# Extra tiles that hold the norm times differences of gamma rows: one conditioning kernel, a new set of tiles for boundary tokens

## The chip, the core and the metric

The kernel runs on one core of a Trainium2 chip. The metric is the device time of one execution in microseconds (us), the median of several runs. The engines of the core work side by side, each through its own queue in order: TensorE (PE, matrix products; PEld is its weight load), VectorE (DVE), ScalarE (ACT), GpSimd (POOL), and SyncE (SP), which here only issues DMAs. POOL issues the indirect DMAs (gathers and scatters), too. An instruction at the head of a queue that waits for another engine or a transfer holds all those behind it.

## The reference

For 8192 tokens (16 batches of 512) of width 512, six vectors are made of each token's row, weighted by a softmax `w`, joined to 3072 columns, and sent through a two-layer perceptron with a norm. `c` is a compartment of 5, `m` a scale type (0 or 1 in the inputs, `mask_BxS_ik0`; the table has 3 rows):

```python
h = _ln(x, pw_g[pathway_ids], pw_b[pathway_ids])        # one of 500 rows
h = _ln(h, cp_g[compartment_ids], cp_b[compartment_ids])
t = _ln(x, tm_g[time_steps], tm_b[time_steps])          # time_steps = the compartment's index
m, n, r = x + cond_1, x + cond_2, x + cond_3            # rows of the batch
s = _ln(x, ms_g[scale_type], ms_b[scale_type])
cat = concatenate([w[0]*h, w[1]*t, w[2]*m, w[3]*n, w[4]*r, w[5]*s])
x = x + _ln(silu(cat @ int_W1 + int_b1) @ int_W2 + int_b2, int_g, int_be)
```

All of it is float32.

## The kernel before, in words

**Sorted tokens.** The kernel numbers the 15 groups (m, c) and sorts the tokens by group on the chip. Rows of x are fetched by gathers and the results scattered back, so a tile of 128 sorted tokens nearly always belongs to one group. 16 windows of 512 tokens (4 tiles) run one after the other. For a tile of one group, gamma of t and of s is one row each, so `t` and `s` share the plain norm `n` of x: `n @ V` with `V = diag(w1 tm_g[c]) W_t + diag(w5 ms_g[m]) W_s`. `s_part` (ACT, piece `sp`) makes the second summand, `build` (DVE, piece `bd`) adds the first, for each tile, into one of two buffers `vs`. The first layer of a tile is then three products of four chunks: `X` (x by `wx_`, the weighted sum of three blocks of `int_W1`), `V`, and `H` (the h path by `wh_`). The second layer is the product with `w2` (`Z`). What depends only on group and batch (betas, conditions, bias) is a row of a table (`rows_1`, `rows_2` in DRAM), gathered into tiles `add` by `i_add` (`gather_add`, piece `ga`) and added to the products in PSUM.

**Turning.** An operand goes through a 32x32 block transpose on DVE (`turn`, tiles `rX`, `rV`, `rH`, `rZ`) and then four DMAs per group of rows on SP (`spread_row`: `cX`, `cV`, `cH`, `cZ`).

**Boundary tokens.** Where a group ends inside a tile, the tile has tokens of two groups. Before the change the tile's V is that of the group that holds position 64 (`middle`), and tokens of the other group have their norm multiplied by 0 (`prim`, used in `x_mean` to make `mrs` and `mnm`, from which `norm_v` makes the masked norm; `norm_n` makes the plain one). The 14 boundaries give 14 half tiles of 64 positions, joined in pairs to `NX` = 7 extra tiles of 128 tokens, held as two extra windows `e0` (tiles 0 to 3) and `e1` (tiles 4 to 6). For them the kernel gathers x again (`gx.e*`), takes its norm, gathers both gamma rows of each token from `pair_rows` (`gather_pair`, `gr`), multiplies (`by_pair`, `mt`: two products a tile), turns both (`turn_pair`, `tr`), spreads both (`sT`, `sS`), multiplies with the weights `wt` and `ws` (`extra`, `ex`: 4 chunks each), adds the group's row of `rows_1` (`extra_add`, `ea`, a gather; `extra_end`, `ee`), and writes the sums behind the table in `rows_2` (`extra_out`, `eo`). Boundary tokens take their row from there. `of_begins`, `begins` and `swap_begins` (`bx`, `by`, `px`) compute where the boundaries lie; `extra_adds` (`xa`) and `add_rows` (`ar`) make the indices.

**The head.** Sorting ends at about 33 us. From there to the last product of window 1's H, and some way into window 2, a written-out sequence `ORDER` sets what every engine's queue gets. Each word is a call, as `lX.0.1` for layer 1, block X, window 0, tile 1. The others that the prediction names: `gh` gathers the h path's rows into `pw` and `cp` (three buffers each); `xs` sums x and its squares on ACT; `xe`, `xp`, `xm` make the norm's factors (DVE, POOL, DVE); `nv`, `xn` the norms; `tv`, `tx`, `tz` turn; `f1`, `fp`, `fm`, `fn`, `f2` are the h path's steps; `wk.s.c` adds a part to `wx_`; `h2`, `he`, `eh`, `cs`, `cp`, `cn`, `ct`, `ca`, `cm`, `cr` make the condition rows; `tb`, `br2` the beta rows (`tb` reads `wh_`, weighted by `wh` and loaded by `lh`); `pk`, `rp`, `rc`, `ro` make and write the table; `sz`, `scl` the scales of the tiles; `ax`, `ac`, `pwi`, `tk` the token indices; `sh` adds a row to x; `ha`, `hs` are the hidden layer's addition and silu; `l2` the Z product. After the head, `step` issues sixteen steps for each of the windows 2 to 14, and `last_window` the last.

Of the kernel before, what the change touches and what calls it, by code (L numbers as in the profile page):

```python
# [23 lines left out]
def kernel(ctx: ExitStack, tc: tile.TileContext, a: dict, out: bass.AP):  # L24
# [73 lines left out]
    prim = const.tile([P, NJ, NW], F32, name="prim")  # L98
# [98 lines left out]
    def x_mean(st):  # L197
        w = st["w"]
        st["nm"] = small.tile([P, NJ], F32, tag="nmx", name="nmx")
        nc.vector.tensor_mul(st["nm"], st["sums"][:, 1], st["rs"])  # L200
        for k in ("rs", "nm"):
            if isinstance(w, int):
                st["m" + k] = m = small.tile([P, NJ], F32, tag="m" + k, name="m" + k)
                nc.vector.tensor_mul(m, st[k], prim[:, :, w])
            else:
                st["m" + k] = st[k]

    def norm(st, j, rs, nm, tag):
        t = xnp.tile([P, D], F32, tag=tag, name=f"{tag}{st['w']}_{j}")
        nc.scalar.activation(t, st["xb"][:, j, :], AF.Identity, bias=st[nm][:, j : j + 1],  # L210
                             scale=st[rs][:, j : j + 1])
        return t
# [9 lines left out]
    def norm_v(st, j):  # L222
        st["xm", j] = norm(st, j, "mrs", "mnm", "xm")
# [4 lines left out]
    def norm_n(st, j):  # L228
        st["xn", j] = norm(st, j, "rs", "nm", "xn")
# [203 lines left out]
    i_half = iota(prep.tile([P, 2, NX], F32, name="i_half"), [[1, 2], [2, NX]])  # L433
# [141 lines left out]
    def half_cols(k):  # L575
# [15 lines left out]
        lambda: nc.gpsimd.tensor_add(half[:, :1], half[:, 1:], i_row[:NB]),  # L591
        lambda: nc.gpsimd.tensor_scalar(slot, i_half[:NB], i_row[:NB], half[:, :1], ALU.is_equal, ALU.mult),
    ]

    def tile_pairs():
        pt = ps_2.tile([P, 2, Q * NW], F32, tag="p2", name="ptp")
        for v, w in enumerate((wcs, wms)):
            nc.tensor.matmul(pt[:NR, v], w[:, :NR], middle, start=True, stop=True)
        p0 = ps_1.tile([P, Q + 1, NW], F32, tag="p1", name="p0")
        nc.tensor.matmul(p0[:, :Q].rearrange("p g w -> p (g w)"), ones[:NB], middle, start=True, stop=True)  # L600
        for g in range(Q):
            nc.tensor.matmul(p0[g * L : (g + 1) * L, Q], ones[:NB, :L], middle[:, g * NW : (g + 1) * NW],
                             start=True, stop=True)
        return pt, p0
# [7 lines left out]
    def row_pairs():  # L612
# [23 lines left out]
    at_c = scratch(0, P)[: Q * NW]  # L636
# [35 lines left out]
    HOME = {"e0T": "Z", "e0S": "X", "e1T": "Z", "e1S": "V"}  # L672
# [8 lines left out]
    def of_rows():  # L681

        at_["pa"] = pa = ps_2.tile([P, 3, Q * NW], F32, tag="p2", name="pa")
        nc.tensor.transpose(pa[:, 0], at_c, ident[: Q * NW, : Q * NW])
        swap(pa[:, 1:].rearrange("p v (j w) -> p j v w", j=NJ), at_n[:, 1:].rearrange("p v g w -> p g v w"), 2 * NW)
# [14 lines left out]
    def of_begins():  # L700

        at_["pnx"] = pnx = ps_2.tile([P, 2, NX], F32, tag="p2", name="pnx")
        H = P // 2
        for k in range(2):
            for h in range(2):
                nc.tensor.matmul(pnx[k * H : (k + 1) * H, 0], at_c[:, h * H : (h + 1) * H], b_at[:, h, k::2],
                                 start=(h == 0), stop=(h == 1))
# [12 lines left out]

# [51 lines left out]
    def rows_of_pw():  # L772
        nc.vector.tensor_scalar(i_pw, both, (1 << PW) - 1, None, ALU.bitwise_and)
        nc.vector.tensor_copy(i_cp.rearrange("p j w -> p (j w)"), at_["pa"][:, 2])
# [406 lines left out]
```

## Time and profile before

| what | us |
|---|---|
| median of 3 runs | 1024.62 |
| lowest and highest run | 1023.46 and 1024.70 |
| span of the profiled execution, first to last instruction | 1018.6 |
| PE busy in it | 987.3 |
| DVE busy | 827.9 |
| ACT busy | 547.2 |
| POOL busy | 554.0 |

The page gives the profiled execution's time only as this span; the runs' median is 6.0 us above it. The mean clock that was granted to PE is 0.991 of full speed. A matrix product of 128 x 128 by 128 x 512 in float32 stands as two instructions, so a tile's product with a 512 x 512 block is 8 of them. "Busy" of PE counts overlapping instructions once. In lines of waits, the engine before the arrow waited for what stands behind it; a row of the order of instructions has its start, its duration, engine, line, operation, operands, shape and count, and in brackets the idle time before it. Line numbers are those of the code above; L137 is `spread_row`, L169 `build`, L163 `s_part`, L278 `layer1`, L297 `layer2`, L890 `extra`, L878 `by_pair`, L103 any gather.

### The profile page before, as it was taken

The numbers are of one execution on the slowest core, as the hardware profiler recorded it, in microseconds if no ns is written. First come the engines' busy times: TensorE is split into PE (matmuls) and PEld (weight loads), VectorE is DVE, ScalarE is ACT, GpSimd is POOL, SyncE is SP. The second block draws the span as 40 slices with busy tenths as digits, with TensorE's granted clock in tenths as the row PEclk, the third lists the DMA queues.
The fourth block names the chain that finished last, engine by engine and source line by source line (L and its number), as shares of the span: only waits on it lengthen the run. The fifth ranks groups of instructions, "written<-read, shape, count | busy, mean of one in ns | idle before, by whom it ended". The sixth has DMA issues, their size and how long they took to land.

```text
span 1018.6 us, 10840 instructions
## 1 busy us (share of the span) xinstructions
PE 987.3 (97%) x2593; PEld 451.2 (44%) x2593; DVE 827.9 (81%) x1442; ACT 547.2 (54%) x1098; POOL 554.0 (54%) x561
## 2 busy tenths in 40 slices
PE   7998989899999999999999999999999999999996
PEld 7733434344444444444444444444444444444442
DVE  8698375888888888889888888888888889888844
ACT  5786634636464554736473746455463747364311
POOL 8437354537464655556564746464655656473514
PEclk9799999999999999999999999999999999999999
DMA  8858776767666666667685766667766768575412
GB/s 285 272 153 277 226 234 169 216 164 231 169 197 180 183 187 198 192 196 202 169 231 158 220 167 198 181 186 188 202 192 193 202 175 226 159 224 162 138 51 91
DMA packets 93505, 194.57 MB, mean 191 GB/s; under 512 B 25712, under 2 KB 25712, under 8 KB 93444
## 3 DMA queue, kind: packets, MB, share of 16 engines
q0 software_dynamic: 32048, 108.81, 36.3%
q1 hardware_dynamic: 60692, 85.00, 30.2%
q8 instruction: 22, 0.36, 0.1%
q14 instruction: 39, 0.32, 0.1%
q10 hardware_dynamic: 704, 0.08, 0.1%
HBM read 104.47 MB, written 19.67 MB: 122 GB/s over the span
## 4 chain that ended last, share of the span: by engine, by line
DVE 45%; DMA 13%; issue 13%; PE 9%; ACT 7%; SPq 6%; POOL 5%; POOLq 0%; DVEq 0%; ACTq 0%
DVE vs L169 13%; SPq L137 6%; DMA cH<-rH 5%; DVE yb L326 4%; DVE add L282 3%; POOL xbs L103 3%; PE p L278 3%; DVE pw L234 3%; DVE pw L262 3%; DVE sth L108 3%; DVE pw L233 3%; PE p L297 2%; PE pe L890 2%; ACT xn L210 2%; DVE rZ L129 2%
## 5 line engine op out<-in xcount | busy, mean ns | idle before, releaser
L297 PE MATMUL p<-w,cZ 128*128 128x512 f32 x512 | 229.0, 592 | 2.1 <-DMA cZ<-rZ 2.1
L278 PE MATMUL p<-vs,cV 128*128 128x512 f32 x504 | 226.8, 593 | 1.9 <-DVE vs L169 1.9
L278 PE MATMUL p<-wh__83,cH 128*128 128x512 f32 x512 | 223.0, 593 | 5.3 <-DMA cH<-rH 5.3
L278 PE MATMUL p<-wx__82,cX 128*128 128x512 f32 x512 | 222.9, 593 | 0.0
L169 DVE SCALAR_TENSOR_TENSOR vs<-wt,sct,vs 128x512 f32<-128x512 f32 x252 | 206.7, 879 | 0.0
L163 ACT ACTIVATE vs<-ws,scs 128x512 f32<-128x512 f32 x252 | 160.5, 707 | 0.3
L242 POOL TENSOR_TENSOR rsh<-veh,mhalf 128x1 f32<-128x1 f32 x64 | 45.7, 713 | 202.6 <-DVE veh L238 191.8
L278 PEld LDWEIGHTS p<-wh__83,cH 128*128 128x128 f32 x512 | 97.0, 190 | 128.6 <-issue 123.9
L297 PEld LDWEIGHTS p<-w,cZ 128*128 128x128 f32 x512 | 97.1, 190 | 125.3 <-issue 120.5
L278 PEld LDWEIGHTS p<-wx__82,cX 128*128 128x128 f32 x512 | 97.0, 190 | 122.7 <-issue 118.3
L278 PEld LDWEIGHTS p<-vs,cV 128*128 128x128 f32 x504 | 94.8, 190 | 124.8 <-issue 92.0
L249 ACT ACTIVATE pw<-pw,nmh,rsh 128x512 f32<-128x512 f32 x64 | 51.8, 810 | 125.3 <-DVE nmh L120 121.2
L285 ACT ACTIVATE add<-add 128x512 f32<-128x512 f32 x64 | 40.4, 631 | 144.9 <-DVE add L282 144.9
L331 POOL DMA_INDIRECT out<-yb,tok x64 | 70.0, 1093 | 71.1 <-DVE yb L326 24.5
L305 ACT ACTIVATE junk<-yb 128x512 f32<-128x512 f32 x64 | 40.1, 627 | 95.9 <-DVE yb L300 95.9
L103 POOL DMA_INDIRECT add<-rows,i_add x64 | 75.6, 1181 | 18.8 <-issue 12.4
L233 DVE TENSOR_TENSOR pw<-xn,pw 128x512 f32<-128x512 f32 x64 | 44.0, 687 | 51.3 <-ACT xn L210 49.0
L103 POOL DMA_INDIRECT xbs<-in_x,tok x64 | 64.4, 1006 | 35.1 <-issue 18.3
L267 POOL TENSOR_TENSOR xbs<-xbs,rows 128x512 f32<-128x512 f32 x64 | 81.5, 1274 | 0.9
L103 POOL DMA_INDIRECT pw<-in_pw,i_pw x64 | 63.8, 996 | 30.6 <-DVE rH L129 13.9
L210 ACT ACTIVATE xm<-xbs,mnm,mrs 128x512 f32<-128x512 f32 x64 | 48.7, 805 | 55.8 <-DVE rV L129 49.1
L103 POOL DMA_INDIRECT cp<-cp_rows,i_cp x64 | 65.1, 1017 | 19.9 <-issue 19.2
(255 smaller groups left out, 1145.2 us busy)
## 6 DMA issues: line engine op xcount, KB each, us to landing
cV<-rV SPq DMA_DIRECT2D x256, 64.0 KB
cH<-rH SPq DMA_DIRECT2D x256, 64.0 KB
cZ<-rZ SPq DMA_DIRECT2D x256, 64.0 KB
cX<-rX SPq DMA_DIRECT2D x240, 64.0 KB
w1x<-in_int_W SPq DMA_DIRECT2D x2, 1024.0 KB
cTe<-rTe SPq DMA_DIRECT2D x28, 64.0 KB
cSe<-rSe SPq DMA_DIRECT2D x28, 64.0 KB
rows<-adde SPq DMA_DIRECT2D x7, 256.0 KB
```

The costliest lines, as they stand in the source:

```text
L103: nc.gpsimd.indirect_dma_start(dst, None, table, bass.IndirectOffsetOnAxis(ap=idx, axis=0), **kw)
L137: nc.sync.dma_start(st[cat][q * L : (q + 1) * L, g].rearrange("p c t -> p (c t)"), st[rot][g * L : (g + 1) * L, q].rearrange("p c j t -> p ...
L163: nc.scalar.activation(v[:, c], ws[:, c], AF.Identity, scale=scs[:, c, g, w : w + 1])
L169: nc.vector.scalar_tensor_tensor(v[:, c], wt[:, c], sct[:, c, g, w : w + 1], v[:, c], ALU.mult, ALU.add)
L210: nc.scalar.activation(t, st["xb"][:, j, :], AF.Identity, bias=st[nm][:, j : j + 1], scale=st[rs][:, j : j + 1])
L233: nc.vector.tensor_mul(pw[:, :D], st.pop(("xn", j)), pw[:, :D])
L242: nc.gpsimd.tensor_tensor(rs, st.pop(("ve", j)), mhalf[:, :1], ALU.pow)
L249: nc.scalar.activation(pw[:, :D], pw[:, :D], AF.Identity, bias=st.pop(("nm", j)), scale=st.pop(("rs", j)))
L267: nc.gpsimd.tensor_add(st["xb"][:, j, :], st["xb"][:, j, :], rows[:, 2, :])
L278: nc.tensor.matmul(st["p1", g], st["c" + blk][:, g, c, :], m[:, c, :], start=(blk == "X" and c == 0), stop=(blk == "H" and c == NC - 1))
L297: nc.tensor.matmul(p2, st["cZ"][:, j, c, :], w2[:, c, :], start=(c == 0), stop=(c == NC - 1))
L331: nc.gpsimd.indirect_dma_start(out_rows, bass.IndirectOffsetOnAxis(ap=tok[:, j, w : w + 1], axis=0), yb[:, j, :], None)
```

## The change

The main V product takes all tokens of the tile with the plain norm, boundary tokens, too; so `prim` and the masked factors go, and one set of factors serves `norm_v` and `norm_n`. For tokens whose group differs from the tile's, the extra tiles now make the correction `n * (gamma row of its own - gamma row of the tile)`. The tokens that differ in compartment need the T block, those that differ in scale type the S block. Seven T tiles take the 14 half tiles, and one S tile takes the two boundaries at which the scale type changes (`b_at[:, :, :2]`). So there are eight extra tiles of one block each, where there were seven of two.

The differences are rows of a small table `diff_rows` (25 pairs of compartments and 9 of scale types), made by one product of `tg` (the eight gamma rows) with a matrix `picks` of +1 and -1 (`dk`, `dp`), copied with the weight (`dc`) and written to DRAM (`do`). `pair_rows` and its six DMAs go. `kinds` (`kd`) computes which pair each extra token has, from its own group and that of its tile (`g_at`, three more products in `row_pairs`).

The S tile (k = 0) is written behind the table in `rows_1`; the T tiles gather from `rows_1` with these rows included, so a token that differs in both adds its S correction to its T tile. `ORDER` is new throughout; of the pieces `prim` is gone, and `kd`, `dk`, `dp`, `dc`, `do` and `sE` come in.

The core of the diff:

```diff
-    rows_1 = dram.tile([NB1, D], F32, name="rows_1")
+    rows_1 = dram.tile([NB1 + P, D], F32, name="rows_1")
-    pair_rows = dram.tile([NG, 2 * D], F32, name="pair_rows")
+    diff_rows = dram.tile([ND, D], F32, name="diff_rows")
...
     def x_mean(st):
         nc.vector.tensor_mul(st["nm"], st["sums"][:, 1], st["rs"])
-        for k in ("rs", "nm"):
-            if isinstance(w, int):
-                st["m" + k] = m = small.tile([P, NJ], F32, tag="m" + k, name="m" + k)
-                nc.vector.tensor_mul(m, st[k], prim[:, :, w])
...
+        pgt = ps_2.tile([P, 3 * (P // 2)], F32, tag="p2", name="pgt")[: Q * NW]
+        nc.tensor.matmul(pgt[:, :P], cols[:, 6], rowed, start=True, stop=False)
+        nc.tensor.matmul(pgt[:, :P], cols[:, 5], ones[:NB], start=False, stop=True)
+        nc.tensor.matmul(pgt[:, P:], cols[:, 7], ones[:NB, : P // 2], start=True, stop=True)
...
+        for v, (src, lo, step) in enumerate(((at_c, 0, H), (g_at, 0, H), (g_at, P, 0))):
+            for k in range(2):
+                for h in range(2):
+                    nc.tensor.matmul(pnx[k * H : (k + 1) * H, v], src[:, lo + h * step :][:, :H], b_at[:, h, k::2],
+                                     start=(h == 0), stop=(h == 1))
...
+    def diff_product():
+        at_["pdr"] = pdr = psum(1, "pdr")[:ND]
+        nc.tensor.matmul(pdr, picks[:, 0], tg, start=True, stop=True)
...
-        st["r", j] = r = gp.tile([P, 2 * D], F32, tag="pw", name=f"pr{st['w']}_{j}")
-        gather(r, pair_rows[:, :], tok_x[:, j, 1, e : e + 1])
+        st["r", j] = r = gp.tile([P, D], F32, tag="cp", name=f"pr{st['w']}_{j}")
+        gather(r, diff_rows[:, :], tok_x[:, j, 1, e : e + 1])
+    def by_diff(st, j):
+        nc.vector.tensor_mul(st["r", j], st.pop(("xm", j)), st["r", j])
+    def turn_diff(st, j):
+        turn_to(st, "rE", HOME[st["w"] + "E"], j, st.pop(("r", j)))
...
-        for v, m in (("cT", wt), ("cS", ws)):
-            for c in range(NC):
-                nc.tensor.matmul(pe, st[v][:, k % Q, c, :], m[:, c, :],
-                                 start=(v == "cT" and c == 0), stop=(v == "cS" and c == NC - 1))
+        for c in range(NC):
+            nc.tensor.matmul(pe, ext[k // Q]["cE"][:, k % Q, c, :], (wt if k else ws)[:, c, :],
+                             start=(c == 0), stop=(c == NC - 1))
...
-        gather(at_["adde", k], rows_1[:, :], i_addx[:, k : k + 1])
+        gather(at_["adde", k], rows_1[: NB1 + (P if k else 0), :], i_addx[:, k : k + 1])
...
-        nc.sync.dma_start(rows_2[NB1 + k * P : NB1 + (k + 1) * P, :], at_["adde", k])
+        if k == 0:
+            nc.sync.dma_start(rows_1[NB1:, :], at_["adde", k])
+        else:
+            nc.sync.dma_start(rows_2[NB1 + (k - 1) * P : NB1 + k * P, :], at_["adde", k])
```

The new order, by queue, over the part from the sorting to the end of window 1's first layer, where the prediction speaks of it:

```
PE:   sz bx ax h2.1 h2.2 cv h2.0 eh.2 eh.0 px eh.1 dp xt.0.2 xt.0.3 xt.0.1 xt.0.0 ct tb cm lX.0.1 lX.0.3 lX.0.0 rp.1 lX.0.2 rp.0
      lV.0.1 lV.0.0 lH.0.1 lH.0.0 lV.0.3 lV.0.2 ex.0 ex.1 lH.0.3 ex.3 ex.2 ex.4 ex.6 ex.7 ex.5 lX.1.2 lX.1.3 lH.0.2 lX.1.0 lX.1.1
      lV.1.0 lV.1.1 lV.1.2 l2.0.1 l2.0.0 l2.0.2 l2.0.3 lV.1.3 lH.1.0 lH.1.1 lH.1.2 lH.1.3
DVE:  ... tk cg cs wk.2.2 xv.0.2 tt wk.2.0 cn xv.0.3 xe.0 xv.0.1 xv.0.0 xm.0 ca f1.0.2 wk.2.1 wk.2.3 fm.0.2 f1.0.0 tv.0.2 f2.0.2 ...
      ... ee.1 ee.2 ee.3 f1.1.3 ee.4 tv.1.1 fm.1.0 ee.6 bd.1.0 tv.1.2 ee.7 ee.5 tv.1.3 fm.1.3 f1.1.2 f2.1.0 fm.1.2 bd.1.1 ...
POOL: gh.0.2 gh.0.0 gh.0.1 cp gx.e1.3 gx.e0.1 gx.e1.2 xp.0 gx.e0.0 fp.0.2 ... gh.1.3 xp.1 ea.2 ea.1 gx.2.1 sh.0.3 ea.4 sh.1.0 ea.3 ea.6
      fp.1.0 gx.2.3 ea.7 fp.1.3 ea.5 sh.0.1 fp.1.2 ga.0.3 ga.0.2 ga.0.1 ga.0.0 ...
SP:   ... sE.e0.3 eo.0 sE.e1.0 sE.e1.2 sE.e1.3 sE.e1.1 eo.2 eo.1 sX.1.2 eo.3 sX.1.3 sH.0.2 sX.1.0 eo.6 eo.4 eo.7 eo.5 sX.1.1 sV.1.1 ...
```

Before, the same stretch of PE's queue was:

```
PE:   h2.1 bx ax sz px h2.0 xt.0.0 xt.0.1 xt.0.2 cv eh.0 xt.0.3 eh.1 h2.2 lX.0.1 eh.2 lX.0.2 lX.0.0 ct lX.0.3 cm tb lV.0.1 rp.0 rp.1
      lV.0.3 lV.0.0 lV.0.2 lH.0.0 lH.0.2 lH.0.1 ex.0 ex.1 ex.3 ex.2 lH.0.3 ex.6 ex.4 ex.5 lX.1.0 ... lX.1.3 lV.1.0 ... lV.1.3
      l2.0.1 l2.0.2 l2.0.0 l2.0.3 lH.1.0 lH.1.1 lH.1.2 lH.1.3
```

More of the change, by code (lines that the diff above doesn't have):

```diff
@@ L23 @@
+"""
 @with_exitstack
@@ L432 @@
     nc.gpsimd.tensor_scalar(i_own, i_own, float(NB1), None, ALU.add)
-    i_half = iota(prep.tile([P, 2, NX], F32, name="i_half"), [[1, 2], [2, NX]])
+    i_sx = prep.tile([P, 1], F32, name="i_sx")
+    nc.gpsimd.tensor_scalar(i_sx, i_row, float(P // 2), float(-(P // 2)), ALU.is_ge, ALU.mult)
+    nc.gpsimd.tensor_add(i_sx, i_sx, i_row)
+    nc.gpsimd.tensor_scalar(i_sx, i_sx, float(NB1), None, ALU.add)
+    picks = prep.tile([P, 2, ND], F32, name="picks")[:NR]
+    for v in range(2):
+        iota(picks[:, v, :ND5].rearrange("p (a b) -> p a b", a=NR5), [[1 - v, NR5], [v, NR5]])
+        iota(picks[:, v, ND5:].rearrange("p (a b) -> p a b", a=NR3), [[1 - v, NR3], [v, NR3]], base=NR5)
+    w_d = prep.tile([P, 1], F32, name="w_d")[:ND]
+    nc.gpsimd.tensor_scalar(w_d, i_row[:ND], float(ND5), None, ALU.is_ge)
     h1 = scratch(1, NC, 3, L)
@@ L598, in tile_pairs @@
             nc.tensor.matmul(pt[:NR, v], w[:, :NR], middle, start=True, stop=True)
[L599 to L603, printed above, removed]
+        p0 = ps_1.tile([P, Q, NW], F32, tag="p1", name="p0")
+        nc.tensor.matmul(p0.rearrange("p g w -> p (g w)"), ones[:NB], middle, start=True, stop=True)
         return pt, p0
@@ L719, in extra_tokens, with diff_picks, diff_copy, diff_out @@
         nc.vector.tensor_scalar(tok_x[:, :, 0], tok_x[:, :, 0], PW, None, ALU.logical_shift_right)
+    def diff_picks():
+        pk = picks[:, 0]
+        nc.vector.tensor_scalar(pk, pk, i_row[:NR], None, ALU.is_equal)
+        nc.vector.scalar_tensor_tensor(pk, picks[:, 1], i_row[:NR], pk, ALU.is_equal, ALU.subtract)
+        dw = small.tile([P, 1], F32, tag="dw", name="dw", bufs=1)[:ND]
+        nc.vector.tensor_sub(dw, wx[:ND, 5:6], wx[:ND, 1:2])
+        nc.vector.scalar_tensor_tensor(w_d, w_d, dw, wx[:ND, 1:2], ALU.mult, ALU.add)
+    def diff_product():
+        at_["pdr"] = pdr = psum(1, "pdr")[:ND]
+        nc.tensor.matmul(pdr, picks[:, 0], tg, start=True, stop=True)
+    def diff_copy():
+        at_["dr"] = gp.tile([P, D], F32, tag="add", name="dr", bufs=4)[:ND]
+        nc.scalar.activation(at_["dr"], at_["pdr"], AF.Identity, scale=w_d)
+    def diff_out():
+        nc.sync.dma_start(diff_rows[:, :], at_["dr"])
     def x_block(s, c):
```

141 lines of the change are left out of this document (86 added, 55 removed).

## The prediction

> **What bounds the kernel now.** I read the page first (the span, the engines' shares, the slices), then the busy time by stretches, then the waits of TensorE (PE) in the first 260 us, then the order of instructions on PE, VectorE (DVE), ScalarE (ACT), GpSimd (POOL) and SyncE's DMA queue (SP) in the head. The page:
>
> ```profile
> span 1018.6 us, 10840 instructions
> PE 987.3 (97%) x2593; PEld 451.2 (44%) x2593; DVE 827.9 (81%) x1442; ACT 547.2 (54%) x1098; POOL 554.0 (54%) x561
> ```
>
> PE leaves only 31 us of the span idle. The stretches say where; the columns are the stretch, PE, PEld, DVE, ACT and POOL busy (instructions), clock, DMA share, GB/s:
>
> ```profile
> 32.40:91.80 59.40, 58.37 (x331) 28.99 (x331) 48.97 (x111) 43.47 (x94) 30.01 (x30) 0.91 0.67 209
> 91.80:107.90 16.10, 10.83 (x25) 4.54 (x26) 7.74 (x19) 9.61 (x25) 11.81 (x12) 1.00 1.04 319
> 107.90:165.80 57.90, 53.32 (x122) 23.31 (x120) 31.42 (x57) 26.96 (x57) 23.57 (x23) 0.97 0.67 197
> 165.80:224.50 58.70, 55.70 (x129) 24.06 (x128) 47.98 (x84) 31.05 (x59) 30.25 (x31) 1.00 0.70 191
> 224.50:960.00 735.50, 734.98 (x1713) 324.50 (x1712) 633.57 (x1079) 407.39 (x793) 418.76 (x398) 1.00 0.68 191
> ```
>
> From 224.5 us on PE runs without a gap: 1713 instructions in 735.5 us, 0.429 us each. The change does not touch that code except for two tiny DVE products a window. So the time moves by what happens to the end of the head, the last H product of window 1 (lH.1.3), which ends here at 224.5. The PE instructions that I use, by start, duration, line and operands:
>
> ```profile
> 36.58 0.39 PE L706 MATMUL pnx<-b_at,room 64*64 64x7 f32 x4
> 37.66 0.36 PE L684 MATMUL pa<-ident,room 64*128 64x64 f32 x1
> 51.03 3.70 PE L278 MATMUL p<-wx__82,cX 128*128 128x512 f32 x8
> 71.78 3.70 PE L278 MATMUL p<-vs,cV 128*128 128x512 f32 x8
> 75.32 1.02 PE L855 MATMUL pr<-br,pick 128*120 128x512 f32 x2
> 80.50 7.03 PE L278 MATMUL p<-vs,cV 128*128 128x512 f32 x16
> 104.35 3.67 PE L278 MATMUL p<-wh__83,cH 128*128 128x512 f32 x8 [3.19 <-DMA cH<-rH]
> 107.86 3.60 PE L890 MATMUL pe<-wt,cTe 128*128 128x512 f32 x8
> 111.29 3.60 PE L890 MATMUL pe<-ws,cSe 128*128 128x512 f32 x8
> 143.50 5.30 PE L890 MATMUL pe<-wt,cTe 128*128 128x512 f32 x8 [4.58 <-DMA cTe<-rTe]
> 148.63 3.60 PE L890 MATMUL pe<-ws,cSe 128*128 128x512 f32 x8
> ```
>
> One product of a 128-token tile with one 512x512 block is 8 instructions and takes 111.29 - 107.86 = 3.43 us. PE's waits in the head (total, times, longest), leaving out those before 33 us, in code that hardly changes:
>
> ```profile
> PE p L278 <- DMA cH<-rH: 5.3, 2, 3.2
> PE pe L890 <- DMA cTe<-rTe: 4.6, 1, 4.6
> PE p L297 <- DMA cZ<-rZ: 2.1, 2, 1.7
> PE p L278 <- DVE vs L169: 1.4, 2, 0.9
> ```
>
> They are 13.4 us. After the longest, 4.58 us, the next eight instructions took 148.63 - 143.50 = 5.13 us instead of 3.43: 1.7 more at a lower clock. So **15.1 us of removable stall** stands in the head.
>
> **The extra products.** Before, seven extra tiles have eight chunk products each (four T, four S), 56 chunks or 14 blocks; after, eight tiles have four each, 8 blocks. Six blocks go: 6 x 3.43 = **-20.6 us**. In 107.9 to 165.8 PE is at 53.3 of 57.9 us, while DVE has 31.4, so these blocks are on the path there, not fillers.
>
> **Added PE work.** `of_begins` goes from 12 small instructions (36.58 to 37.66, 1.1 us, 0.09 each) to 24: 1.1. `row_pairs` gets three small products, 6 instructions: 0.6 at that pace. `diff_product` is one product of 512 columns, 2 instructions of 0.43: 0.9. `p0` loses eight tiny ones, between 0 and 0.7; I take 0.1. Together **+2.5 us**.
>
> **DVE, SP and POOL work on the extra tiles.**
>
> ```profile
> L878 DVE SCALAR_TENSOR_TENSOR pre<-xme,wx,pre x16: 709/746/752, 83.5 to 135.7; 128x512 f32<-128x512 f32 x16
> L129 DVE STREAM_TRANSPOSE rTe<-pre x8: 669/702/711, 86.1 to 136.4; 128x512 f32<-128x512 f32 x8
> L137 SPq DMA_DIRECT2D cTe<-rTe x28: 507/582/606, 98.1 to 151.9; - x28
> ```
>
> Of 16 products and 16 transposes half go: 8 x (0.75 + 0.70) = 11.6 us of DVE; about twenty small new ones (`kinds`, `diff_picks`, `extra_adds`), each at most the 0.23 of the small cast below, give up to 4.6 back. SP loses 56 - 32 = 24 spread issues, 24 x 0.6 = 14 us, and the six `pair_rows` ones. The gathers of pairs halve (8 x 256 KB less). The head's DVE load (136.1 us in the first four stretches) becomes (136.1 - 7.0)/169.3 = 76% (the head then lasts from 32.4 to 201.7, below), under the 86% (633.57/735.5) that the steady part bears, and the 3.7 MB less help the stretch 91.8 to 107.9, where the DMA share is 1.04. I cost these at nothing: they are what removes the two waits for cH and cTe.
>
> **POOL and SP before 35 us.** POOL gets some thirteen more small operations (iotas, index arithmetic).
>
> ```profile
> 35.17 1.24 POOL L103 DMA_INDIRECT xbs<-in_x,tok  x1 [9.41 <-PE p L602]
> 40.49 0.95 POOL L103 DMA_INDIRECT pw<-in_pw,i_pw  x1 [0.30 <-issue]
> 41.74 0.95 POOL L103 DMA_INDIRECT cp<-cp_rows,i_cp  x1 [0.30 <-issue]
> 54.87 1.05 POOL L191 TENSOR_TENSOR rsx<-vea,mhalf 128x4 f32<-128x4 f32 x1 [6.07 <-DVE vea L187]
> ```
>
> POOL's 9.41 us of idleness before its first gather hides them, up to 0.7 us each; without that cover they would delay the first gathers by their own sum. On SP six `pair_rows` issues go ahead of the loads of `lt` and `lh`, which can only help.
>
> ACT and DVE rows for the next two steps:
>
> ```profile
> 46.85 0.63 ACT L181 ACTIVATE junk<-xbs 128x512 f32<-128x512 f32 x1
> 48.69 0.63 ACT L181 ACTIVATE junk<-xbs 128x512 f32<-128x512 f32 x1
> 60.16 0.80 ACT L210 ACTIVATE xn<-xbs,nmx,rsx 128x512 f32<-128x512 f32 x1
> 73.98 2.55 ACT L163 ACTIVATE vs<-ws,scs 128x512 f32<-128x512 f32 x4
> ```
>
> ```profile
> 39.59 0.23 DVE L774 CAST i_cp<-pa 128x64 int32<-128x64 f32 x1 [1.48 <-ACT at_n L698]
> 61.26 0.65 DVE L233 TENSOR_TENSOR pw<-xn,pw 128x512 f32<-128x512 f32 x1
> 63.61 0.15 DVE L238 TENSOR_SCALAR veh<-mvh 128x1 f32<-128x1 f32 x1
> ```
>
> **The new order, first stage: window 0's X products start later.** Before, they begin at 51.03. In the new order `ct`, `tb` and `cm` stand ahead of lX.0.1 on PE, and `wk.2.1 wk.2.3` (the last parts of wx_) stand on DVE behind `f1.0.2`. Followed by rows: `sz` (2 us) and the longer `bx` run ahead of `ax`, so i_cp comes at about 42 instead of 39.8, and the six gathers `gh.0.*` (1.25 apart) start at 42.5. The second's `cp` buffer is that of `tg`, which `dp` still reads until about 50, so they end at 53.7. Behind them on POOL: `cp`, three gathers of extra x (3.8), then `xp.0` (1.05), done at 59.2 (before: 55.9). Then `xm.0` and `xn.0.2` 0.9, `f1.0.2` 2.5 (61.26 to 63.76), two `wk` 1.5 (as L878, 0.75 each): 64.1, and as products go chunk by chunk lX.0.1 starts at about 63.5. Behind it 13.7 (X) and 5.2 (`rp`, 80.50 - 75.32): V starts at 82.4. Before, with `rp` counted ahead as well, 71.78 + 5.2 = 77.0. That is 5.4 later, 2.5 of it the added work: **+2.9**. V's operand is ready just then: on DVE two more `f1.0` (5.0), `f2.0.2` and four transposes (6 x 0.7) bring tv.0.3 to 73.3; two groups of four spreads 4.8, landing 4.4 (the chain's row further down): 82.5.
>
> **Second stage: sp.0.3 is late.** Before, it ran at 73.98. Now ACT has, from `sp.0.0` (42 us, when `ac` has its rows) on, twelve sums `xs` (1.84 each: 48.69 - 46.85), sixteen norms `nv`, `xn` and `fn` (0.8), `sp.0.0`, `sp.0.1` and `sp.0.3` itself (2.55), `wh` (2), and eight copies (0.6): 22.1 + 12.8 + 7.7 + 2 + 4.8 = 49.4. That ends at 91.4 if ACT never waits; I add 7 for its waits on `xp.0`, `fp` and the two buffers of norms, 98.5. PE reaches lV.0.3 at 82.4 + 4 x 3.43 = 96.1 and starts it with the first built chunk, at about 99: **+3.0** (0 without the waits).
>
> **Third stage: a new wait.** The seven T tiles gather their rows from `rows_1`, whose last 128 rows the S tile writes (`eo.0`). So `ea.2` holds POOL until that write lands, and behind it on POOL stand `ea.1`, `gx.2.1`, `sh.0.3` and the other `ea`; DVE waits at `ee.1`, and PE's ex.6 needs the PSUM bank that `ee.1` frees. The chain shows such links:
>
> ```profile
> 139.00 4.41 DMA cTe<-rTe
> 167.80 3.37 DMA rows<-adde
> 175.97 4.67 DMA add<-rows,i_add
> ```
>
> From ex.0's end: `ee.0` 0.7, issue 0.6, landing 3.4, two gathers 2.5, landing 4.7, `ee.1` 0.7: 12.6 us. PE has ex.1, lH.0.3, ex.3, ex.2 and ex.4 before ex.6: 17.2. 4.6 us are spare: cost 0. But `add` tiles have four buffers: ea.6 waits for eo.2's landing, ea.5 for eo.4's, which on SP stands behind eo.6. By the same links: ex.2 ends at 82.4 + 3.0 + 11 x 3.43 = 123.1; `ee.2` and `eo.2` 1.3, landing 3.4; ea.6 1.25 and 4.7; `ee.6`, `eo.6` and `eo.4` 1.9, landing 3.4; ea.5 1.25 and 4.7; so ee.5 comes at about 145.7, 8 us after ex.5's end (136.8) and the addition would allow it, and behind it on DVE stands `tv.1.3`, behind eo.5 on SP the spread of V, behind its landing the gathers `ga.0.*`. PE has window 1's X products (13.7) to do meanwhile, then I reckon 2 us of waiting before its V, 1.5 before window 0's Z products and 1 before H: **+4.5**. Ends: 0, if the buffers come free in time, and 15.1, as much stall as the head has now.
>
> **Sum.** -20.6 + 2.5 - 15.1 + 2.9 + 3.0 + 4.5 = -22.8: lH.1.3 would end at 201.7. Against the execution's own span: 1018.6 - 22.8 = 995.8. The median of the runs, 1024.6, is 6.0 above the span, for what lies around it, so the forecast is **1001.8**. All three added stalls at 0: 1024.6 - 33.2 = 991.4. The old stalls kept in full beside the new early one: 1009.4.
>
> The clock: a wait of 3.19 us (at 104.35) left the next block at 107.86 - 104.35 = 3.51 us, one of 4.58 was followed by 5.13. The Trainium skill, "TensorE: Matmul & The Clock Gate", Part 1, says that the gate halves the clock after an idle window of about 3.4 us, and restores it after as long a busy one; the rows agree. By that rule the thin work ahead of lX.0.1 (gaps of about 2, 1.5 and 1 us, between `xt`, `ct`, `tb` and `cm`) costs nothing unless they run together; if they do, the sum would be 1.7 worse, 1003.5.
>
> **Rivals.** (a) *The stalls only change place.* Every stage has a queue that I followed only at its longest wait; others may stand in the place of the old ones. For it: the first stage is worse than now, and 91.8 to 107.9 shows transfers at full share. Against: SP loses 14 us of issues exactly where cTe was awaited. 1009.4, up to 1020 with 10 more lost.
> (b) *The extra products were filler.* If the head ended by DVE, ACT and transfers whatever PE does, the six blocks would turn into idle time: 1024.6. Against: PE is 92% busy in that stretch, and DVE idles.
> (c) *The S tile's rows hold the head: slower.* The place is `ea.2` on POOL. It decides when the loop from ex.0 to `ee.1` exceeds 17.2 us by more than the 22.8 gained, i.e. takes over 40 us instead of 12.6. Both landings at the slowest of a gather here, 9.45 (below), give 23.4: 6.2 us of PE stall, 1008. A queue that stands still for another reason would have to add 16.6; then 1025 and more, 1030 with 5 on top.
>
> ```profile
> 99.78 9.45 DMA xbs<-in_x,tok_x
> ```
>
> **How the numbers follow.** The forecast's case (991 to 1009) 0.68; (a), beyond 1009, 0.20; (b) 0.04; (c), slower, 0.08. The bound of no change is 0.2%, 2 us, about what the three runs can tell. Faster 0.68 + 0.20 = 0.88, same 0.04, slower 0.08. From the low end of the sum, 991.4, and half of case (a), 1014, the range is 991 to 1014; about 0.2 lies outside.
>
> **What would show it.** PE about 18 us less busy (969); L890's group at 64 instructions; lX.0.1 at 60 to 66 us and lH.1.3's end at 198 to 206; no wait of PE for cE, but waits for `vs` and for cV or cZ; POOL waiting at the gather of `adde` for `rows`. Wrong: an end of lH.1.3 beyond 215, a PE wait at L890 for the PSUM bank, or idle time of PE after 225 us.

## The result and the profile after

| kernel | median us (lowest to highest) | runs | ratio to before, 95% interval |
|---|---|---|---|
| before, same chip | 1024.04 (1021.93 to 1024.70) | 4 | 1 |
| after | **989.44** (989.26 to 993.01) | 4 | 0.9674 [0.9654, 0.9694] |

The change takes 34.6 us off, a gain of 3.3%. Forecast were 1001.8 us and a range of 991 to 1014: the direction was right, and the gain was 12 us larger than forecast, 1.6 us past the range's end.

The page of after, its first lines and its chain:

```profile
span 987.2 us, 10703 instructions
PE 964.4 (98%) x2557; PEld 441.8 (45%) x2557; DVE 803.8 (81%) x1413; ACT 548.6 (56%) x1101; POOL 561.8 (57%) x571
...
PE 93%; DVE 4%; issue 1%; DMA 1%; another core or an unknown queue 0%; ACT 0%; POOL 0%; POOLq 0%
```

PE lost 22.9 us of work and the span 31.4, so 8.5 us of PE's idle time went too (slow products count as busy). The busy time by stretches of after (same columns as before):

```profile
32.40:60.00 27.60, 22.99 (x227) 13.01 (x228) 15.67 (x52) 16.95 (x44) 17.05 (x16) 0.82 0.68 211
60.00:90.00 30.00, 30.00 (x109) 13.47 (x102) 28.40 (x66) 27.56 (x62) 15.94 (x18) 0.99 0.63 200
90.00:110.00 20.00, 20.00 (x48) 8.82 (x47) 15.35 (x32) 16.57 (x37) 14.21 (x15) 1.00 0.94 279
110.00:150.00 40.00, 40.00 (x95) 17.57 (x94) 27.70 (x50) 24.90 (x53) 23.03 (x23) 1.00 0.83 250
150.00:189.00 39.00, 38.58 (x91) 16.96 (x90) 35.80 (x62) 22.77 (x39) 22.91 (x21) 1.00 0.66 188
```

From 60 to 150 us PE has no gap at all, though DVE is at 71.45 of 90 us and the DMA engines at 0.94 in one stretch. PE's order of instructions in after (start, duration, operands, count, idle time before):

```profile
54.32 0.66 PE L795 MATMUL pt<-ident,xbs 128*128 128x128 f32 x4 [1.73 <-DVE cX L800]
56.43 0.55 PE L884 MATMUL pt<-ident,room 96*128 96x96 f32 x4 [1.45 <-DVE cX L800]
56.91 1.93 PE L851 MATMUL pbt<-wt,room 128*32 128x512 f32 x8
58.62 1.88 PE L851 MATMUL pbt<-ws,room 128*32 128x512 f32 x8
60.33 1.03 PE L851 MATMUL pbt<-wh__83,room 128*32 128x512 f32 x8
...
63.87 10.57 PE L299 MATMUL p<-wx__82,cX 128*128 128x512 f32 x24
82.89 7.03 PE L299 MATMUL p<-vs,cV 128*128 128x512 f32 x16
96.62 7.03 PE L299 MATMUL p<-vs,cV 128*128 128x512 f32 x16
113.78 20.86 PE L955 MATMUL pe<-wt,cEe 128*128 128x512 f32 x48
193.51 7.03 PE L299 MATMUL p<-wx__82,cX 128*128 128x512 f32 x16
```

The head's end, the start of window 2's X products, moved from 224.51 to 193.51: -31.0 of the span's -31.4. From there on the kernel takes what it took (794.1 us before, 793.7 after). L955 is `extra` in after: six of its eight tiles run as one block of 48 instructions, where before it had the wait of 4.58 us for `cTe`.

The account of the 31.0, from the same rows: V's start 82.89 against 71.78 + 5.2 (`rp`) is +5.9; six blocks fewer, -20.6. From V's start to the head's end lay 38 blocks of 3.43 us (24 of the two windows and 14 extra ones) and `rp` before, in 152.73 us, so 17.2 of it were stall, waits and slow products together; after, 32 blocks lie in 110.62, so 0.9 are: -16.3. Together -31.0. This accounts for the two profiled executions. The 3.2 us by which the medians differ more (34.6 - 31.4) lie in executions of before that were not profiled.

### The profile page after: what moved, and what is told of

Read it like the earlier page. It is cut to its first block, busy times and chain, and to the rows that moved or that the text cites. A ratio compares the mean times of both kernels' runs of the same rounds, so it can differ in the third digit from the quotient of the medians.

```text
span 987.2 us, 10703 instructions
## 1 busy us (share of the span) xinstructions
PE 964.4 (98%) x2557; PEld 441.8 (45%) x2557; DVE 803.8 (81%) x1413; ACT 548.6 (56%) x1101; POOL 561.8 (57%) x571
## 4 chain that ended last, share of the span: by engine, by line
PE 93%; DVE 4%; issue 1%; DMA 1%; another core or an unknown queue 0%; ACT 0%; POOL 0%; POOLq 0%
PE p L299 67%; PE p L318 21%; PE pe L955 3%; DMA out<-yb,tok 1%; DVE vs L570 1%; PE pbt L851 0%; DVE vs L574 0%; DVE yb L321 0%; DVE vs L572 0%; PE pb L894 0%; PE hs L821 0%; ACT vs L191 0%; DVE xbs L570 0%; DVE vs L503 0%
## 5 line engine op out<-in xcount | busy, mean ns | idle before, releaser
L197 DVE SCALAR_TENSOR_TENSOR vs<-wt,sct,vs 128x512 f32<-128x512 f32 x252 | 194.2, 829 | 0.3 <-issue 0.3
L131 POOL DMA_INDIRECT add<-rows,i_add x64 | 71.9, 1124 | 14.9 <-issue 13.8
L131 POOL DMA_INDIRECT pw<-in_pw,i_pw x64 | 68.0, 1063 | 18.0 <-issue 14.0
L339 POOL TENSOR_TENSOR rsy<-vey,mhalf 128x4 f32<-128x4 f32 (+1 forms) x22 | 24.3, 1106 | 57.3 <-DVE vey L334 57.0
```

The lines of the kernel that those rows point to most:

```text
L131: nc.gpsimd.indirect_dma_start(dst, None, table, bass.IndirectOffsetOnAxis(ap=idx, axis=0), **kw)
L197: nc.vector.scalar_tensor_tensor(v[:, c], wt[:, c], sct[:, c, g, w : w + 1], v[:, c], ALU.mult, ALU.add)
```

## The experiments

Each ratio is to runs of the kernel before on the same chip. In kernels with lines added, the same code stands one to six lines lower than in after; e2's lines are those of before plus 28.

**The two halves of the change, each alone: e1_old_order and e2_new_order.** e1 is the changed arithmetic (eight one-block tiles) in the old `ORDER`; e2 is the old arithmetic in the new `ORDER`.

```diff
e1: -ORDER of after
    +ORDER of before; no prim; kd dk behind by; dp dc do behind px; sT.* become sE.*, no sS.*;
    +ea.2 ea.3 ea.1 behind eo.0; ex.7 ea.7 ee.7 eo.7 behind ex.5 ea.6 ee.5 eo.5; sE.e1.3 behind sE.e1.1
e2: -ORDER of before
    +ORDER of after; no kd dk dp dc do and no tile 7; prim behind pwi; each sE.* becomes sT.* sS.*; sT.e0.3 ahead of tr.e1.0;
    tv.1.0 nv.1.2 behind sS.e1.1
```

> The new extra tiles (eight of one block) with the old order of the head, changed only where it must be: prim out, the new pieces in, sE in the places of sT, the T tiles' gathers ea.1 to ea.3 behind eo.0, and ex.7, ea.7, ee.7, eo.7, sE.e1.3 added behind their neighbours. Theory: six blocks less on PE are 6 x 3.43 = -20.6 us, +2.5 of added work, and the old order keeps much of its stall (15.1 to 17.1 us): about 1024 - 18 = 1006, between 998 and 1014; the new order's share is then 10 to 25 us. Rival (the extra products were filler, the order brings all the gain): within 3 us of the kernel before. Rival (the products bring all, the order nothing): within 3 us of 989.4.

> The old extra tiles (seven of two blocks, the masked norm) with the new order of the head, changed only where it must be: each sE is sT and sS, prim in, the new pieces and tile 7 out, sT.e0.3 ahead of tr.e1.0, tv.1.0 and nv.1.2 behind sS.e1.1. Theory: the new kernel's 989.4 + 20.6 for six blocks - 2.5 for the small work = 1007.5 if the new order leaves PE no stall here either; up to 1015 because 24 more spread issues of 0.6 us and pairs of twice the size come late. Rival (the order alone brings the gain): 989 to 993. Rival (the order works only with the smaller tiles): 1020 to 1030.

Measured: e1 1020.0 (1017.48 to 1021.42, 7 runs), ratio 0.9952 [0.993, 0.9974]; e2 1024.78 (1022.76 to 1026.78, 10 runs), ratio 1.0003 [0.9983, 1.0023]. So the parts alone bring some 4 us and nothing, and both together 34.6. Neither expectation of the main theory held: e2 came out as its second rival had it, e1 just outside its first (filler). The account of the 31.0, made for all four profiled executions (start of window 0's V; blocks of 3.43 us and stall from there to the start of window 2's X; `rp`'s 5.2 counted as ahead of V in all):

| kernel | V's start, against before | blocks | stall | head's end, against before |
|---|---|---|---|---|
| before | 71.78 | 38 | 17.2 | 224.51 |
| after | 82.89, +5.9 | 32 | 0.9 | 193.51, -31.0 |
| e1 | 80.25, +8.5 | 32 | 30.4 | 225.57, +1.1 |
| e2 | 84.79, +7.8 | 38 | 13.1 | 228.20, +3.7 |

In e1 the six blocks go, but the start is 8.5 us later and the stall grows by 13.2, with 20.95 of its 30.4 at one place; PE's order, DVE's and SP's:

```profile
80.25 3.70 PE L300 MATMUL p<-vs,cV 128*128 128x512 f32 x8
...
150.41 16.17 PE L956 MATMUL pe<-wt,cEe 128*128 128x512 f32 x32 [20.95 <-DMA cEe<-rEe]
...
225.57 13.90 PE L300 MATMUL p<-wx__82,cX 128*128 128x512 f32 x32
...
130.52 0.69 DVE L964 TENSOR_TENSOR adde<-pe,adde 128x512 f32<-128x512 f32 x1 [7.32 <-DMA adde<-rows,i_addx]
141.38 0.69 DVE L948 TENSOR_TENSOR pre<-xme,pre 128x512 f32<-128x512 f32 x1 [5.16 <-DMA pre<-diff_rows,tok_x]
142.88 2.42 SPq L166 DMA_DIRECT2D cEe<-rEe  x4
```

PE stands 20.95 us for the spread of a T tile. DVE had been held by `ee.1`, which waits 7.32 us for rows that include the S tile's (the link that the prediction's third stage named), and stood again for a gamma gather that POOL issued late; only then could the operand be turned and spread. In the old order `ee.1` stands ahead of that last turn, in the new one behind all the T tiles' turns. In e2, with seven two-block tiles in the new order, PE is busy 25.5 us longer than in after (989.9 for 964.4) and waits besides; its waits, and two rows of its order:

```profile
PE pe L918 <- DVE adde L926: 3.3, 1, 3.3
PE pt L849 <- issue: 3.3, 1, 3.3
PE pe L918 <- DMA cTe<-rTe: 2.5, 1, 2.5
...
84.79 7.03 PE L306 MATMUL p<-vs,cV 128*128 128x512 f32 x16
228.20 13.90 PE L306 MATMUL p<-wx__82,cX 128*128 128x512 f32 x32
```

**Whether the old order's loss is one chain: e5_old_order_gr.** e1 with the late gather and its predecessor early, and the held additions behind the spread:

```diff
-mt.e1.0 ... ee.1 ... eo.1 ... tr.e1.0 ... gr.e1.3 ... ee.3 ... eo.3 ... sE.e1.2
+mt.e1.0 tr.e1.0 gr.e1.3 ... sE.e1.2 ee.1 eo.1 ee.3 eo.3
```

> The new tiles in the old order, as e1_old_order, with one chain shortened: tr.e1.0 and the gather gr.e1.3 directly behind mt.e1.0, and ee.1, eo.1, ee.3, eo.3 behind the spread sE.e1.2, so that neither POOL nor DVE is held by an extra tile's sum before the last difference tile is turned. In e1_old_order PE waited 20.9 us for cE there. Theory (this chain of queues, not the products or PE, set the time there, so the blocks that went were filler in the old order): the wait falls to 4 to 8 us, 1020 - 15 = 1005, between 1001 and 1010. Rival (the wait has another cause, or returns at the next place): above 1014.

Measured: 1015.9 (1015.18 to 1016.85, 5 runs), ratio 0.9913 [0.9881, 0.9946]. PE's waits at that place:

```profile
139.59 5.31 PE L956 MATMUL pe<-wt,cEe 128*128 128x512 f32 x8 [12.43 <-DMA cEe<-rEe]
```

The wait fell from 20.95 to 12.43 and a second one of 2.64, and a new wait of 2.8 for `cX` came, while those for `cV`, `cZ` and `cH` (1.5, 1.6 and 1.6 in all) stayed. And of the 5.7 us between the two profiled spans (1018.6 and 1012.9), 3.7 lie ahead of the first V (76.53 for 80.25), where the two orders are the same; so the edit is worth about 2 us there. The rival came true: the loss of the old order is several queue places, not one chain. What holds the remaining 12.43 was not followed further.

**Whether PE is the path in the changed kernel: e3_twice.** The extra products are made twice, 8 more blocks of the same operands:

```diff
-        for c in range(NC):
+        for c in 2 * list(range(NC)):
             nc.tensor.matmul(pe, ext[k // Q]["cE"][:, k % Q, c, :], (wt if k else ws)[:, c, :], ...
```

> The new kernel with each extra tile's four chunk products made twice into the same sum, so that the corrections come out doubled: eight blocks of 3.43 more on PE and nothing else. Theory (PE has no stall behind which they could hide): 989.4 + 27.5 = 1017, at least 1013. Rival (room elsewhere in the head takes some up): below 1008.

Measured: 1016.15 (1015.84 to 1016.62, 5 runs), ratio 0.9924 [0.9894, 0.9955]: +26.7 for 27.5 of work. So in the new order, a block there costs its full time. That settles rival (b) for the new order: there the extra products are no filler. In the old order (b) was nearly true, as e1 shows: of the 20.6 us that the six blocks leave, 13.2 come back as stall.

**The first stage: e4_head, e6_sp00, e7_warm, e9_warm_wk, e10_wk.** What holds lX.0.1 at 63.87? e4 puts the index work ahead of `sz` and rearranges PE's and DVE's work before lX.0.1 (in part as in the old order); e6 takes `sp.0.0` off ACT's early queue; e7 fills PE's two waits ahead of `ct` with two unread products; e10 puts the last two parts of `wx_` ahead of `f1.0.2` on DVE; e9 does e7 and e10.

```diff
e4:  -sz scl bx lt ax wk.1.3 h2.1 ac sp.0.0 ... ct ... tb br2 fp.0.2 cm do xn.0.0 wk.2.3 lX.0.1
     +bx ax wk.1.3 lt wk.1.1 by pwi sz ac kd dk scl h2.1 ... xp.0 wh lX.0.1 ct ... lX.0.3 f1.0.2 ... tb br2 fp.0.2 cm do xn.0.0 sp.0.0
e6:  -ac sp.0.0 ... sp.0.1
     +ac ... sp.0.1 sp.0.0
e7:  +    t = psum(0, ...); nc.tensor.matmul(t, ident, wt[:, n, :], start=True, stop=True)   # behind xt.0.1, and behind xt.0.0
e10: -f1.0.2 ... wk.2.1 ... wk.2.3
     +wk.2.1 wk.2.3 f1.0.2 ...
```

> The new kernel with another order of the pieces before window 0's V: bx and ax ahead of sz, dp right behind h2.1 and px, sp.0.0 behind the sums xs.0, wk.2 ahead of f1.0.2, two X products ahead of ct, tb and cm. Theory: what is left of stall and low clock between 39 and 64 us (waits of 1.0, 1.7 and 1.5 us, 2.7 us until at_n is copied, tb's products at half pace) is worth about 4.9 us against PE's bare work; this order takes 2 to 5 of it: 985 to 987.5. Rival (V's operand, spread from 73 us on and needed at 83, becomes the wait instead): 988 to 991.

> The new kernel with sp.0.0 moved on ACT from ahead of the condition copies (he) to behind sp.0.1. The copies, the sums xs.0, wh and with them tb and lX.0.1 come about 2 us earlier, sp.0.1 and bd.0.1 unmoved, bd.0.0 has 2.5 us less room. Theory (PE has no stall behind lX.0.1): 989.4 - 2 = 987.4, between 986 and 988.5. Rival (V's operand or bd.0.0 comes late instead, nothing gained): 989 to 991.

> The new kernel with two more products of 128x128 by 128x512 whose results nobody reads, in PE's two waits (1.7 and 1.5 us) ahead of ct. Nothing else changes. Theory (the products of tb run at half pace, 4.4 us in place of 2.6, because PE was thinly used in the 10 us before): they run at full pace, -1.8, at most -2.5: 987 to 988. Rival (the clock does not come back by two products, or they delay ct by their own 0.9 to 1.7 us each): 989 to 991.5.

> The changed kernel with wk.2.1 and wk.2.3 ahead of f1.0.2 on VectorE, nothing else. Theory: TensorE's own tb and cm at the lower clock end at 63.9 and hold lX.0.1, so nothing moves: lX.0.1 at 63.7 to 64.1, 988.8 to 990.5. Rival, as the prediction's first stage reckoned (lX.0.1 held by f1.0.2 and then the two parts of wx_): lX.0.1 at about 62.5, 987.5 to 988.5.

> Two unread products in TensorE's waits ahead of ct, as in the kernel that ran with them before (988.97), and now the last two parts of wx_ (wk.2.1, wk.2.3; 1.4 us on VectorE) ahead of f1.0.2 as well, in VectorE's wait of 1.3 us for the norm's scales. Theory: in that run TensorE itself (tb, cm) held lX.0.1 at 63.3, so the parts of wx_ are not what is awaited: lX.0.1 at 63 to 63.6, 988 to 990. Rival: wx_ is awaited: lX.0.1 at 62.2 to 62.8, 987 to 988.

| run | median us (lowest to highest, runs) | ratio | lX.0.1 starts |
|---|---|---|---|
| e4 | 1002.46 (1001.13 to 1004.35, 6) | 0.9785 [0.9759, 0.9811] | 61.92 |
| e6 | 991.19 (989.60 to 992.35, 6) | 0.9672 [0.9646, 0.9697] | 63.78 |
| e7 | 988.97 (987.87 to 989.64, 6) | 0.9652 [0.9627, 0.9677] | 63.31 |
| e10 | 990.80 (988.99 to 1000.51, 6) | 0.9675 [0.9654, 0.9696] | 63.96 |
| e9 | 991.52 (988.97 to 991.86, 5) | 0.9677 [0.9656, 0.9697] | 64.01 |

e4 was a miss by 15 us: X starts 2 us sooner, but PE waits ahead of X for the copies of `cX` and ahead of V for `cV`, which it does not in after, and the products behind both waits are slow (6.63 us for one block, 8.80 for two). V starts 11.6 us later than in after:

```profile
61.92 6.63 PE L300 MATMUL p<-wx__82,cX 128*128 128x512 f32 x8 [3.98 <-DVE cX L801]
94.50 8.80 PE L300 MATMUL p<-vs,cV 128*128 128x512 f32 x16 [2.74 <-DMA cV<-rV]
```

e6, expected to bring 2 us, moved lX.0.1 by 0.1, as its rival had it; PE's wait of 1.45 us ahead of `ct` stayed. e7 was to show the clock. In after `tb`'s first two groups took 1.93 and 1.88 us, with waits of 1.73 and 1.45 ahead of them (rows above); with the two fillers:

```profile
57.15 1.06 PE L857 MATMUL pbt<-wt,room 128*32 128x512 f32 x8
58.03 1.04 PE L857 MATMUL pbt<-ws,room 128*32 128x512 f32 x8
...
60.59 1.06 PE L900 MATMUL pb<-yb,room 128*32 128x512 f32 x8 [0.67 <-PE pbt L857]
```

The 1.7 us of slow products are gone, but `cm` then waits 0.67 us for the copy of `pbt`, and lX.0.1 starts only 0.56 sooner. That the fillers did it is not shown: e3, whose code is that of after up to here, has the same two waits, no fillers and the full pace, with lX.0.1 at 63.12:

```profile
54.37 0.66 PE L795 MATMUL pt<-ident,xbs 128*128 128x128 f32 x4 [1.73 <-DVE cX L800]
56.48 0.55 PE L884 MATMUL pt<-ident,room 96*128 96x96 f32 x4 [1.45 <-DVE cX L800]
56.96 1.06 PE L851 MATMUL pbt<-wt,room 128*32 128x512 f32 x8
```

So one execution to the next differs there as much as e7 from after. With `wx_` ready sooner (e10, and e9 beside the fillers) the start does not come earlier; in both, lX.0.1 follows PE's own `cm` without a wait (e9's execution had lost 0.7 us ahead of `ct` already, and its median, 991.52, lies above both of its expectations). The prediction's chain over `f1.0.2` and the parts of `wx_` gave the right time (63.5), but PE's own `tb` and `cm` end there too; what would move the start was not found. No version here is measurably faster than the changed kernel; e7's 988.97 lies within its scatter.

**The second stage: e11_sp03_late.** ACT makes `sp.0.3` three times over, so that it is as late as the prediction had it:

```diff
-        for c in range(NC):
+        for c in (3 if w == 0 and g == 3 else 1) * list(range(NC)):
             nc.scalar.activation(v[:, c], ws[:, c], AF.Identity, scale=scs[:, c, g, w : w + 1])
```

> The changed kernel with the four scalings of sp.0.3 done three times over (the same values), so that ScalarE has it done at about 98.9 instead of 93.8, the lateness that the prediction gave it. Theory: the products go chunk by chunk and TensorE is at 96.6 when it wants the tile, so it waits only for the first of the four chunks, 1.0 to 1.5 us, and VectorE's and ScalarE's delay of 5 us is made up elsewhere: 990.5 to 992. Rival, the prediction's step: 2.4 to 3.0 us at this place, 992 to 993. Second rival: the queues of ScalarE and VectorE hold no slack and the delay comes out again in the third stage: over 993.5.

Measured: 992.13 (990.79 to 993.82, 5 runs), ratio 0.9693 [0.9674, 0.9713], 2.7 above after. ACT's and PE's rows:

```profile
91.04 7.46 ACT L191 ACTIVATE vs<-ws,scs 128x512 f32<-128x512 f32 x12
...
97.50 3.70 PE L299 MATMUL p<-vs,cV 128*128 128x512 f32 x8 [0.71 <-issue]
101.37 3.70 PE L299 MATMUL p<-vs,cV 128*128 128x512 f32 x8 [0.16 <-issue]
...
127.44 10.57 PE L955 MATMUL pe<-wt,cEe 128*128 128x512 f32 x24 [1.77 <-DVE adde L963]
```

At its own place, ACT's end at 98.5 costs PE only 0.9 us, since the products go chunk by chunk and the first chunk is built long before the last is scaled. A further 1.77 us comes at 127.44, in the third stage: PE wants the bank that `ee.1` frees. Together they make 2.6 of the 2.7. So the median stands in the first rival's range, but the rival's 2.4 to 3.0 us did not come at its place; most of the loss is what the second rival named.

**The third stage: e8_eo_late.** The write of the S tile's rows goes behind the spreads of e1 on SP, and the two gathers behind it on POOL follow it:

```diff
-eo.0 ... ea.2 ... ea.1 ... sE.e1.0 ... sE.e1.2 ... sE.e1.3 ... sE.e1.1
+sE.e1.0 ... sE.e1.2 ... sE.e1.3 ... sE.e1.1 eo.0 ea.2 ea.1
```

> The new kernel with the write of the S tile's rows (eo.0) behind the spreads sE.e1 on SP, some 14 us later, and ea.2, ea.1 behind it on POOL, as the data demand. Theory (the S tile's rows have some 3 to 5 us of room, then PE's ex.6 waits for the PSUM bank that ee.1 frees, and the queues behind ee.1 with it): +6 to +14, 996 to 1003, with a PE wait at ex. Rival (the rows are not on any path to PE): within 1.5 us of 989.4.

Measured: 998.25 (996.55 to 999.44, 4 runs), ratio 0.9748 [0.9715, 0.9781]. As expected, PE waits where rival (c) placed it:

```profile
130.73 12.66 PE L956 MATMUL pe<-wt,cEe 128*128 128x512 f32 x24 [5.27 <-DVE adde L964]
```

The three blocks behind it took 12.50 us instead of 10.3, so the wait and the slow products account for the 7.4 us between the profiled spans (994.6 and 987.2). The same wait came unasked in one execution of e10, the 1000.51 (its other five lie between 988.99 and 992.7); that one was profiled:

```profile
117.76 0.63 ACT L989 ACTIVATE junk<-w 128x512 f32<-128x512 f32 x1 [2.87 <-remote]
120.00 0.63 ACT L989 ACTIVATE junk<-w 128x512 f32<-128x512 f32 x1 [1.52 <-ACT junk L989]
122.25 0.63 ACT L989 ACTIVATE junk<-w 128x512 f32<-128x512 f32 x1 [1.53 <-remote]
...
126.89 0.69 DVE L255 TENSOR_TENSOR pw<-xn,pw 128x512 f32<-128x512 f32 x1 [10.31 <-ACT xn L232]
...
132.23 13.59 PE L956 MATMUL pe<-wt,cEe 128*128 128x512 f32 x24 [6.13 <-DVE adde L964]
```

Here the rows of the S tile were not late. ACT stood several times between the small sums over `w2`, without another engine of this core that the profile names; so the norm `xn` was late, DVE held 10.31 us at the product with it, and `ee.1`, which stands behind that product on DVE, freed PE's PSUM bank 8 us later than in after. So the third stage's place is real and its room small; how often an execution runs into it was not counted.

## Why the prediction was right, and where it was wrong

**Right.** The bound (PE's head, then a steady part that does not change) and the sizes of its two large terms: the six blocks at full price (e3: 26.7 for eight), and the old stalls gone, though this term was too small: 17.2 where 15.1 were counted. The waits are 13.4 of it; the other 3.8 are blocks that took longer than 3.43 us, of which the prediction had counted only the one behind the longest wait, 1.7. The first stage came out nearly at its time: lX.0.1 at 63.87 (63.5), V at 82.89 (82.4), so +5.9 for +2.5 and +2.9. That was in part luck: the chain followed, to the parts of `wx_`, ends at 64.0, but PE's own `cm` ends at 63.9, and with `wx_` ready sooner (e10) the start stays. Of the signs, PE's busy time (964.4 for 969), L955's group at 64 instructions, no wait for `cEe`, and no idle time of PE behind the head came; the head's end came at 193.5, ahead of the 198 to 206, and the waits for `vs`, `cV` and `cZ` did not come.

**The clock ahead of lX.0.1.** The granted clock is 0.82 in the stretch 32.4 to 60, and two groups of `tb` ran at half pace behind gaps of 1.73 and 1.45 us with 0.66 us of work between them; in e3 they ran at full pace behind the same gaps. The Trainium skill, "TensorE: Matmul & The Clock Gate", Part 1, has a free-running activity window of about 3.4 us; that after and e3 differ behind the same gaps agrees with a window that does not start with the work. How little work in a window counts as idle is not shown here. The price was 0.75 us at lX.0.1 (63.87 against e3's 63.12), not the 1.7 that the prediction named, since without the half pace `cm` waits for the copy of `pbt`, 0.66 us in e3.

**Wrong: "Second stage", +3.0.** It cost 0. ACT's row of `sp.0.3` in after, and DVE's `build` of it:

```profile
91.24 2.56 ACT L191 ACTIVATE vs<-ws,scs 128x512 f32<-128x512 f32 x4
...
92.88 2.72 DVE L197 SCALAR_TENSOR_TENSOR vs<-wt,sct,vs 128x512 f32<-128x512 f32 x4
```

It ended at 93.8, not at 98.5: the 7 us that the step added for ACT's waits were 2.4 in the end. And the step took the last chunk's end for the first chunk's: with ACT's end at 98.5, e11 shows 0.9 us at that place.

**Wrong: "Third stage", +4.5.** It cost 0.9 at most, all the stall that is left behind V's start; ahead of window 1's V PE waits 0.42 us, and ahead of window 0's Z and window 1's H not at all. Two of its links were wrong. POOL's gathers of `rows` and SP's writes in after:

```profile
114.54 1.01 POOL L131 DMA_INDIRECT adde<-rows,i_addx  x1 [0.19 <-issue]
128.66 1.38 POOL L131 DMA_INDIRECT adde<-rows,i_addx  x1 [5.46 <-DVE pw L254]
133.86 1.00 POOL L131 DMA_INDIRECT adde<-rows,i_addx  x1 [0.18 <-issue]
...
107.84 0.35 SPq L967 DMA_DIRECT2D rows<-adde  x1
124.65 0.87 SPq L969 DMA_DIRECT2D rows<-adde  x2
137.38 3.48 SPq L969 DMA_DIRECT2D rows<-adde  x4
```

`ea.2` (114.54) finds the S tile's rows landed: POOL is busy with other gathers until then, so the expected wait isn't there. And `ea.5` (133.86) is issued before `eo.4` (137.38): it does not need `eo.4`'s buffer, but, by the times, the one that `eo.3` (128.14) frees; that fits a ring whose buffers go to the next gather in the order in which they come free. Only `ea.6` waits, 5.46 us on POOL, by its time for the landing of `eo.2` (124.65), though the row names DVE; nothing that PE needs soon is behind it. At the first link the prediction had 4.6 us to spare, and there it was too generous: from ex.0's end (106.9) to `ee.1`'s the loop took 17.1 us, not 12.6. DVE's row of `ee.1` and `ee.2` in after:

```profile
123.34 1.29 DVE L963 TENSOR_TENSOR adde<-pe,adde 128x512 f32<-128x512 f32 x2 [0.34 <-DMA adde<-rows,i_addx]
```

`ee.1` ends at about 124.0, and PE takes ex.6 at 113.78 + 3 x 3.43 = 124.1. The room is 0.1 us, and e8, e11 and one execution of e10, which were later there, all fell in.

**Wrong: the 6.0 us around the span.** The median of before's runs was set against the span of another execution. Each timed run lists its own span: over the 41 runs of before in the experiments, time less span is 1.7 to 1.8 us (after: 1.9 to 2.7), while the spans themselves go from 1017.9 to 1028.2, median 1022.3. The profiled execution of before, with 1018.6, was one of its quickest; that of after, 987.2, lies within its four (986.6 to 991.1). The sum's result should have carried 2 us for what lies around the span, and the medians fell by more than the profiled spans: 34.6 for 31.4. What makes most executions of before longer than the profiled one was not tried; the mean clock falls with the span, from 0.991 at 1017.9 to 0.980 at 1028.2.

Of the 12.4 us of error, this step is 3.8 (6.0 less 989.4 - 987.2), the second stage 3.0, the third 3.6, the old stalls 2.1 (17.2 - 15.1) and the tail behind the head 0.4; the first stage goes the other way by 0.5.

## What to carry to other kernels

A written-out order and the work it orders have to be judged together: here each alone brought next to nothing, and both 3.3%, because freed TensorE time is only worth something if the operands reach TensorE on time. Before pricing a late tile, follow it by chunk (the first chunk's time, not the last's), and follow a ring of buffers by who frees one first. And add to a predicted span only what the same execution has around its span, never the difference to the median of others.

## What the runs showed of the hardware

- The pace behind the same thin work can differ from one execution to the next: behind waits of 1.73 and 1.45 us with 0.66 us of products between them, the first group of `tb` took 1.93 us in after, 1.63 in e11 and 1.06 in e3. With two products of 128x512 put into the waits it took 1.06 (e7) and 1.07 (e9).
- ACT can stand for microseconds without another engine of the core that the profile names: three times in the execution of e10 above, which was 10 us over that kernel's median, and ahead of one copy in after:

```profile
39.63 0.36 PE L717 MATMUL pa<-ident,room 64*128 64x64 f32 x1
...
43.91 0.21 ACT L731 COPY at_n<-pa 128x64 f32<-128x64 f32 x1 [4.74 <-remote]
```

The last product into `pa`'s bank that PE's rows show ahead of the copy ends at 41.3, 2.6 us before. This stop is no chance one: in the profiles of e2, e3 and e6 to e11, which keep this part of the order, the copy starts at 43.6 to 44.1, though the last product ends anywhere from 39.8 to 42.0. The cause of either stop was not found.
